# An edge network's segment sum: the row of place numbers written by TensorE into half a bank, and the comparison moved ahead

## The chip, the core and the metric

The kernel runs on one core of one Trainium2 chip. The core has TensorE (PE; its weight loads are shown as PEld), VectorE (DVE), ScalarE (ACT), GpSimd (POOL) and the queues that start transfers, SyncE's (SP) above all. The metric is the device time of one execution in microseconds, the median of several runs. [...]

## The reference

`reference` is one layer of a graph network over 12500 nodes and 212500 edges. Cut to what matters:

```python
h = jnp.maximum(_layernorm(x, axis=-1), 0.0)
edge_in = jnp.concatenate([h[row], h[col], dist], axis=1)
e = jax.nn.silu(edge_in @ eW1 + eb1)
e = jax.nn.silu(e @ eW2 + eb2)
agg = jax.ops.segment_sum(e, row, num_segments=h.shape[0])
node_in = jnp.concatenate([h, agg], axis=1)
out = x + jax.nn.silu(node_in @ nW1 + nb1) @ nW2 + nb2
```

In the call `row` is `src`, in random order of nodes, and `col` is `dst`, by which the edges are sorted.

## The kernel before, in words

**Two halves that overlap.** The first half takes the edges in their order, 208 blocks of 1024. For each block it forms the part of the first product that belongs to `dst` (matmul `qp`, line 459), copies it on ACT into `qs` together with a number (line 477), and POOL sends each 128 rows to a place in a DRAM table `q` that is ordered by the bucket of `src` (line 484). There are 100 buckets of 125 nodes; the places are counted on DVE and PE (`count`, lines 376 to 441: `oh`, `each`, `mine`, `rank`, `to` on DVE, `counts` on PE). A row of `q` has 144 columns: 128 of data and, in column 128, the edge's place: the number of its `src` node within the bucket, 1 to 125, or 0 for an empty row.

The second half reads `q` in steps. A step is four tiles of 128 edges, one of each of four neighbouring buckets; there are 18 levels of 25 steps, 450 in all. The tile `qt` of a step is loaded by SP in `fetch` (line 535), from a pool `ld2` of four buffers. A step's work, by function:

- `s_lr` (567): PE takes the place column of each of the four tiles, spread over 125 columns as the stationary operand, against the identity `identb`. The result, `lr`, has the edges' places along its columns, the same on all 125 partitions: four float32 pieces of 128 columns that fill one bank.
- `s_one_t` (576): DVE compares `lr` with the partition's number, giving `oneT` (node by edge).
- `s_pt` (581): PE transposes `qt` into `pt` and adds the rows `a` of the first product that belong to `src`, picked by `oneT`; ACT applies the first silu (`e1`).
- `s_bias`, `s_p2` (616, 622): ACT puts the second bias in PSUM, PE adds the second product, ACT applies silu (`e2`).
- `s_one` (600): DVE compares the node numbers `nodes1` (in SBUF) with the place column of `qt`, giving `one` (edge by node). At its end it calls `fetch` for four steps later.
- `s_seg` (632): PE sums `e2` over the edges of each node, with `one`, into the only bank `seg`; `s_add` (641) adds it on DVE to `aggT`.

**The order is written by hand.** PE, DVE, ACT and SP run exactly in the order of the program. The list `turn` (line 657) gives it: in turn k the functions are called one after another for steps k plus the number beside them. `None` is a hook, where pieces of the first half (three a block), the node products and the last nodes' work are woven in.

```python
turn = [
    (s_pt, 1), (s_add, -2), (s_one_t, 2), None, (s_bias, 1), (s_p2, 0), (s_one, 0), None, (s_seg, -1), None, (s_lr, 3), None,
]
```

So `lr` of a step comes three turns ahead of its number, `oneT` two, `pt` one, and `one` in its own turn, followed by `seg` a turn later. `lr`, `pt`, `qp` and other short-lived results share the pool `mm` of four banks, in the order in which they are asked for. A tile's buffer goes to its next user when its last reader is done; SP's load of `qt` waits in SP's order for that.

**Kept rows.** The rows `a` are held in SBUF for as many groups of four buckets as fit: `FIRST_KEPT` names those that are kept from their making on, and groups up to `LAST_KEPT` are loaded once and kept. The others are loaded anew at each level (`a`, line 557).

Of the kernel before, what the change touches and what calls it, by code (L numbers as in the profile page):

```python
# [28 lines left out]
F32 = mybir.dt.float32  # L29
F16 = mybir.dt.float16  # L30
BF16 = mybir.dt.bfloat16
# [7 lines left out]
P = 128  # L39
L = 125  # L40
# [11 lines left out]
G = 4  # L52
W = 144
# [6 lines left out]
ROWS = ENDS[-1]  # L60
CAP = ROWS // P
FIRST = 4
FIRST_KEPT, LAST_KEPT = (0, 2, 5, 7, 10, 12, 15, 17, 20, 22), 24
ZP, ZB = 96, 5
FILL0, FILL_EACH, FILL_LATE = 18, 2, 8
AFTER = mybir.DependencyInfo(mybir.DependencyClass.Sync, mybir.DependencyReason.DATA)
# [8 lines left out]
def tile_gnn(ctx: ExitStack, tc: tile.TileContext, x, src, dst, ew, eW1, eb1, eW2, eb2, nW1, nb1, nW2, nb2, out):  # L75
    nc = tc.nc
    N, D = x.shape
    H = eW2.shape[0]
# [9 lines left out]
    const = ctx.enter_context(tc.tile_pool(name="const", bufs=1))  # L88
# [40 lines left out]
    identb = const.tile([P, P], BF16, name="identb")  # L129
# [7 lines left out]
    nodes_i = const.tile([P, L], I32, name="nodes_i")  # L137
# [5 lines left out]
    nodes1 = const.tile([P, L], F32, name="nodes1")  # L143
# [34 lines left out]
    nc.vector.scalar_tensor_tensor(same, plus, -1e6, same, op0=OP.mult, op1=OP.add)  # L178
    ones = const.tile([1, P], F32, name="ones")
    nc.vector.memset(ones, 1.0)  # L180
    before = const.tile([P, P], BF16, name="before")
    nc.vector.tensor_scalar(before, ahead_i, 0.0, float(G), op0=OP.is_gt, op1=OP.mult)
    rest = const.tile([P, P], BF16, name="rest")
# [113 lines left out]
    wk = ctx.enter_context(tc.tile_pool(name="wk", bufs=2))  # L297
# [3 lines left out]
    with ExitStack() as work:  # L301
        mm = work.enter_context(tc.tile_pool(name="mm", bufs=4, space=PSUM))
# [202 lines left out]
        def send_all(s0, s1):  # L505

            for s in range(s0, s1):
                load(s + 2)
                i, rest = divmod(s - FILL0, FILL_EACH)
                if rest == 0 and 0 <= i < len(fills):  # L510
                    fill(*fills[i])

                for j, _ in enumerate(itertools.zip_longest(send(s), count(s + 1))):
                    pending[needed[s]] -= j == PIECES - 1
                    yield
# [3 lines left out]
        steps = [(w, B, n, g) for w, B, n in batches for g in range(n)]  # L519
        PIECES = 1 + TB // G  # L520
        pending = [needed.count(w) for w in range(len(LEVELS))]
        batch, st = {}, {}
# [3 lines left out]
        def fetch(i):  # L526
            if i >= len(batches):
                return
            c, B, n = batches[i]
            assert not any(pending[: c + 1])  # L530
            while B not in done_a:
                next(feed)
            at = B * G * ROWS + G * (ENDS[c] - n * P)
            qt = ld2.tile([P, G * most, W], F32, name="qt")
            ins = nc.sync.dma_start(
                qt[:, : G * n, :].rearrange("p j w -> p (j w)"),
                q[at : at + G * n * P, :].rearrange("(p j) w -> p (j w)", p=P),
            ).ins
            for later in range(c + 1, len(LEVELS)):
                tc.declare_no_dep(ins, group=f"rows{later}", reason="these ranks were full before")  # L540
            tc.add_manual_dep(ins, last_rows[LEVELS[c][1] - 1].name, AFTER)
            tc.add_to_no_dep_group("loads", ins)
            if c == len(LEVELS) - 1 and not ndp:
                kept.clear()
                keeping.close()
                holding.close()
                for name, bufs in (("nd_in", NQ + 5), ("nd", 2), ("al", NQ)):
                    ndp.append(work.enter_context(tc.tile_pool(name=name, bufs=bufs, side="right")))
            a = kept.get(B)
            if a is None:  # L550
                if lap and not ndp and B <= LAST_KEPT:
                    a = kept[B] = lap[0].tile([P, G, H], F32, name=f"al{B}")
                elif ndp:
                    a = ndp[2].tile([P, G, H], F32, name="a_last")
                else:
                    a = ld2.tile([P, G, H], F32, name="a", bufs=NQ - 1)
                nc.sync.dma_start(a, ta_buckets[:, B * G : B * G + G])
            batch[c, B] = [qt, a, None]
            if c == len(LEVELS) - 1:
                node_in[B] = nodes_in(B, ndp[0])  # L560

        def of(k):

            c, B, n, g = steps[k]
            return batch[c, B], [((g * G + t) % n * G + (g * G + t) // n, (g * G + t) // n) for t in range(G)]

        def s_lr(k):
            (qt, _, _), tiles = of(k)
            loc = qt.rearrange("p j w -> p (j w)").bitcast(BF16)
            lr = mm.tile([P, G, P], F32, name="lr", tag="mm")  # L570
            for t, (j, _) in enumerate(tiles):
                at = 2 * (j * W + H) + 1
                nc.tensor.matmul(lr[:L, t, :], loc[:, at : at + 1].to_broadcast([P, L]), identb, start=True, stop=True)  # L573
            st[k] = {"lr": lr}

        def s_one_t(k):
            oneT = wk.tile([L, G, P], F32, name="oneT")
            nc.vector.tensor_scalar(oneT, st[k].pop("lr")[:L], part1[:L, :], None, op0=OP.is_equal)  # L578
            st[k]["oneT"] = oneT

        def s_pt(k):

            (qt, a, _), tiles = of(k)
            oneT = st[k].pop("oneT")
            pt = mm.tile([P, G, P], F32, name="pt", tag="mm")
            for t, (j, _) in enumerate(tiles):
                nc.tensor.matmul(  # L587
                    pt[:, t, :], qt[:, j, :H], ident, is_transpose=True, start=t == 0, stop=False, skip_group_check=True
                )
            for b, same in itertools.groupby(range(G), lambda t: tiles[t][1]):  # L590
                same = list(same)
                cols = slice(same[0], same[-1] + 1)
                nc.tensor.matmul(  # L593
                    pt[:, cols, :], a[:L, b, :], oneT[:, cols, :], start=False, stop=True, skip_group_check=True
                )
            e1 = wk.tile([P, G, P], F32, name="e1")
            nc.scalar.activation(e1, pt, AF.Silu)  # L597
            st[k]["e1"] = e1

        def s_one(k):  # L600
            (qt, _, _), tiles = of(k)
            c, B, n, g = steps[k]
            wide = [P, G // n, n, L]
            loc = qt[:, : G * n, H : H + 1].rearrange("p (j b) w -> p b j w", b=G)
            one = wk.tile([P, G, L], F32, name="one")
            nc.vector.tensor_tensor(  # L606
                one.rearrange("p (b j) l -> p b j l", j=n),
                nodes1[:, None, None, :].to_broadcast(wide),
                loc[:, tiles[0][1] : tiles[0][1] + G // n].to_broadcast(wide),
                op=OP.is_equal,  # L610
            )
            st[k]["one"] = one
            if g == n - 1:
                fetch(c * (NB // G) + B + NQ)

# [25 lines left out]
        def s_add(k):  # L641
# [13 lines left out]


        turn = [
            (s_pt, 1), (s_add, -2), (s_one_t, 2), None, (s_bias, 1), (s_p2, 0), (s_one, 0), None, (s_seg, -1), None, (s_lr, 3), None,
        ]
        hooks = sum(1 for s in turn if s is None)  # L660
        def norm(xs, n, early=False):
# [279 lines left out]
        for _ in range(2):  # L941
            p2 = p2p.tile([P, G, H], F32, name="p2")
            nc.tensor.matmul(p2, ones, b2r, start=True, stop=True)
            nc.scalar.copy(b2f, p2)
        ld2 = work.enter_context(tc.tile_pool(name="ld2", bufs=NQ))
        ndp, lap = [], []
        pieces = send_all(2 * FIRST, nblocks)
        LEAD = 3 * PIECES
# [12 lines left out]
        for w in range(1, len(LEVELS)):  # L961
            start = w * (NB // G) - NQ
# [3 lines left out]
        at = 0  # L966
        for k in range(first, len(steps) + 2):
            for s in turn:
                if s is None:
# [13 lines left out]
                    if tails:  # L983
                        both = tails[at % 2 :: 2][:1] if len(tails) > 1 else tails[:1] * (at % 2)
# [153 lines left out]
```

## Time and profile before

| | |
|---|---|
| median of 3 runs | 3019.96 us (3005.09 to 3024.86) |
| the profiled execution: its own time | 3021.01 us |
| the profiled execution: its span | 3019.2 us |
| mean granted TensorE clock in it | 0.857 |
| PE's share of the chain that ended last | 47% |
| steps; PE matmul instructions | 450; 17391 |

The profile is of one execution. In a row of a group stand the line, the engine, the operation, what it writes and reads, its shape and count; then the busy time of all of them together in us and the mean of one in ns; then the engine's idle time just before them and what ended most of it. Matmuls overlap, so busy time over count is less than the mean. A float32 matmul has two records. The chain of waits is followed back from the last instruction: each piece is what the next one waited for, so a group's share of it is what would be felt if the group took longer. "issue" in it is time in which nothing that the profile shows was waited for. A row of the list of waits reads: engine, line, what ended the wait, then us in total, how often, and the longest; SPq is SP's transfer queue. A row of the timeline or of the chain by time begins with its start and its duration in us.

### The profile page before, as it was taken

Reading aid. Unit: us, or ns where it says so; the run is one execution under the profiler, and the core shown is the slowest. Engines: PE = TensorE matmul, PEld = TensorE weight load, DVE = VectorE, ACT = ScalarE, POOL = GpSimd, SP = SyncE. Lnnn points to the kernel's source line nnn. Section 1 sums busy time; section 2 is a strip of 40 time slices with the busy share of each in tenths; the row PEclk is TensorE's granted clock in tenths of the full one; section 3 lists DMA queues with packets and bytes.
Section 4 is the critical chain, followed back from the end, with each engine's and each line's share of the span. In section 5 each row is a group of like instructions: output and inputs, shape, how many; then the busy total and the mean of one; then the engine's idle time right before and its main releaser. Section 6 shows DMA issues by size and latency. Waiting matters only on the chain.

```text
span 3019.2 us, 48740 instructions
## 1 busy us (share of the span) xinstructions
PE 2356.1 (78%) x17391; PEld 2089.8 (69%) x17391; DVE 1876.5 (62%) x3250; ACT 1096.6 (36%) x2428; POOL 1702.2 (56%) x1712
## 2 busy tenths in 40 slices
PE   2754777778788788888877877887878887878998
PEld 1543566667777777677776767777767776768898
DVE  7653555666667666666665666666666666666555
ACT  2432333333334343333333333333333333434443
POOL 5666556656555555556565665665655556655310
PEclk8555778889989898988898989898888899989999
DMA  4545555444444344444444434444443333333374
GB/s 104 179 156 166 165 177 158 140 133 139 121 125 135 122 139 136 130 127 133 128 142 122 137 120 132 138 136 128 141 131 118 99 110 104 110 99 108 94 226 128
DMA packets 244985, 402.85 MB, mean 133 GB/s; under 512 B 49516, under 2 KB 143647, under 8 KB 244529
## 3 DMA queue, kind: packets, MB, share of 16 engines
q1 hardware_dynamic: 151717, 217.57, 24.5%
q0 software_dynamic: 53536, 123.03, 11.9%
q10 hardware_dynamic: 39482, 59.04, 6.7%
q8 instruction: 140, 2.29, 0.3%
q14 instruction: 110, 0.90, 0.1%
HBM read 192.46 MB, written 207.01 MB: 132 GB/s over the span
## 4 chain that ended last, share of the span: by engine, by line
PE 47%; issue 9%; another core or an unknown queue 8%; DVE 8%; POOL 4%; ACT 2%; DMA 1%; DVEq 0%; POOLq 0%; ACTq 0%; SPq 0%
PE seg L639 10%; PE pt L593 10%; PE p L625 10%; PE pt L587 5%; PE qp L459 5%; POOL q L484 4%; PE lr L573 3%; DVE aggT L650 2%; DVE oneT L578 1%; DVE one L606 1%; DVE mine L434 1%; ACT e L597 1%; DMA qt<-q 1%; PE z L279 1%
## 5 line engine op out<-in xcount | busy, mean ns | idle before, releaser
L484 POOL DMA_INDIRECT q<-qs,to x1661 | 1671.4, 1006 | 1171.5 <-ACT qs L477 655.7
L597 ACT ACTIVATE e<-pt 128x512 f32<-128x512 f32 x450 | 269.4, 599 | 1210.9 <-remote 424.9
L650 DVE TENSOR_TENSOR aggT<-aggT,seg 128x500 f32<-128x500 f32 x425 | 285.7, 672 | 616.7 <-remote 266.3
L639 PE MATMUL seg<-one,e 128*128 128x125 f32 x3600 | 545.9, 297 | 118.5 <-DVE aggT L650 49.5
L625 PE MATMUL p<-w,e 128*128 128x128 f32 x3600 | 564.6, 300 | 62.9 <-issue 53.5
L639 PEld LDWEIGHTS seg<-one,e 128*128 128x128 f32 x3600 | 493.2, 211 | 169.9 <-issue 133.5
L625 PEld LDWEIGHTS p<-w,e 128*128 128x128 f32 x3600 | 508.8, 214 | 100.6 <-issue 83.7
L578 DVE TENSOR_SCALAR oneT<-lr,part 125x512 f32<-125x512 f32 x450 | 335.8, 746 | 114.8 <-remote 29.6
L459 PE MATMUL qp<-win,pick 64*128 64x256 f32 x1662 | 326.3, 461 | 95.2 <-issue 53.4
L629 ACT ACTIVATE e<-p 128x512 f32<-128x512 f32 x450 | 269.8, 599 | 289.2 <-remote 115.0
L587 PE MATMUL pt<-ident,qt 128*128 128x128 f32 x1800 | 311.3, 297 | 35.1 <-issue 23.4
L593 PE MATMUL pt<-oneT,al 125*128 125x128 f32 x1944 | 303.7, 300 | 34.2 <-issue 33.4
L473 ACT COPY qs<-qp 128x512 f32<-128x512 f32 x416 | 243.5, 585 | 216.8 <-PE qp L459 73.0
L459 PEld LDWEIGHTS qp<-win,pick 64*128 64x128 f32 x1662 | 189.4, 214 | 168.8 <-issue 111.7
L593 PEld LDWEIGHTS pt<-oneT,al 125*128 125x128 f32 x1944 | 276.5, 216 | 42.0 <-issue 41.9
L606 DVE TENSOR_TENSOR one<-nodes,qt 128x500 f32<-128x500 f32 x450 | 303.6, 675 | 0.0
L434 DVE TENSOR_TENSOR mine<-oh,counts 128x800 f32<-128x800 bf16 x208 | 204.2, 982 | 159.8 <-remote 90.9
L619 ACT COPY p<-b2f 128x512 f32<-128x512 f32 x450 | 268.4, 596 | 0.0
L587 PEld LDWEIGHTS pt<-ident,qt 128*128 128x128 f32 x1800 | 214.2, 154 | 57.7 <-issue 41.9
L593 PE MATMUL pt<-oneT,ae 125*128 125x128 f32 x1360 | 212.2, 294 | 43.1 <-issue 41.9
L573 PEld LDWEIGHTS <-qt 128*125 128x125 bf16 x1800 | 176.8, 150 | 85.7 <-issue 72.7
L573 PE MATMUL lr<-identb,qt 128*125 128x128 bf16 x1800 | 196.0, 234 | 45.7 <-issue 21.8
(156 smaller groups left out, 1826.7 us busy)
## 6 DMA issues: line engine op xcount, KB each, us to landing
qt<-q SPq DMA_DIRECT2D x450, 288.0 KB
q<-zeros ACTq DMA_DIRECT2D x70, 720.0 KB
q<-qs,to POOLq DMA_INDIRECT x1661
bc<-dests SPq DMA_DIRECT2D x103, 128.0 KB
win<-tb SPq DMA_DIRECT2D x416, 30.0 KB
tb<-got SPq DMA_DIRECT2D x25, 256.0 KB
a_last<-ta SPq DMA_DIRECT2D x25, 256.0 KB
zd<-zn SPq DMA_DIRECT2D x25, 250.0 KB
```

What stands on the lines that cost most here:

```text
L459: nc.tensor.matmul(qps[i][:, t, : n_of[t]], pick[at, t * P : (t + 1) * P], win[at, : n_of[t]], start=True, stop=True)
L484: ins = nc.gpsimd.indirect_dma_start(out=q[:], out_offset=bass.IndirectOffsetOnAxis(ap=to[:k, j : j + 1], axis=0), in_=qs[:k, t, a, :], in ...
L573: nc.tensor.matmul(lr[:L, t, :], loc[:, at : at + 1].to_broadcast([P, L]), identb, start=True, stop=True)
L578: nc.vector.tensor_scalar(oneT, st[k].pop("lr")[:L], part1[:L, :], None, op0=OP.is_equal)
L587: nc.tensor.matmul(pt[:, t, :], qt[:, j, :H], ident, is_transpose=True, start=t == 0, stop=False, skip_group_check=True)
L593: nc.tensor.matmul(pt[:, cols, :], a[:L, b, :], oneT[:, cols, :], start=False, stop=True, skip_group_check=True)
L597: nc.scalar.activation(e1, pt, AF.Silu)
L606: nc.vector.tensor_tensor(one.rearrange("p (b j) l -> p b j l", j=n), nodes1[:, None, None, :].to_broadcast(wide), loc[:, tiles[0][1] : ti ...
L625: nc.tensor.matmul(p2[:, t, :], e1[:, t, :], w2, start=False, stop=t == G - 1, skip_group_check=True)
L629: nc.scalar.activation(e2, p2, AF.Silu)
L639: nc.tensor.matmul(item[2][:, b, :], e2[:, t, :], one[:, t, :], start=j < G, stop=j >= G * (n - 1))
L650: nc.vector.tensor_tensor(v, v, seg, op=OP.add)
```

## The change

Three things are done. In `s_lr` the four matmuls become transposes whose output is bfloat16, so that `lr` takes half of its bank, and a fifth matmul, of one row of ones against one row with the numbers 1 to 125 (`onesb`, `rowb`), writes the node numbers into the other half, as float32, the same on all partitions: `row`. `s_one` is called from `s_one_t`, right after `oneT`, so two steps earlier than before; it reads `row` in place of `nodes1` and has a pool of four buffers, `onep`, in place of two. The call of `fetch` stays where it was, in a function of its own, `s_fetch`. To make room, group 22 is no longer kept from its making on, and group 24 is no longer kept at all.

```diff
-FIRST_KEPT, LAST_KEPT = (0, 2, 5, 7, 10, 12, 15, 17, 20, 22), 24
+FIRST_KEPT, LAST_KEPT = (0, 2, 5, 7, 10, 12, 15, 17, 20), 23
...
+    onesb = const.tile([1, P], BF16, name="onesb")
+    nc.vector.memset(onesb, 1.0)
+    rowb = const.tile([1, L], BF16, name="rowb")
+    nc.vector.tensor_copy(rowb, nodes_i[:1, :])
...
         def s_lr(k):
             (qt, _, _), tiles = of(k)
-            loc = qt.rearrange("p j w -> p (j w)").bitcast(BF16)
-            lr = mm.tile([P, G, P], F32, name="lr", tag="mm")
+            both = mm.tile([P, G * P], F32, name="lr", tag="mm")
+            lr, row = both[:, : 2 * P].bitcast(BF16).rearrange("p (t e) -> p t e", t=G), both[:, 2 * P : 2 * P + L]
             for t, (j, _) in enumerate(tiles):
-                at = 2 * (j * W + H) + 1
-                nc.tensor.matmul(lr[:L, t, :], loc[:, at : at + 1].to_broadcast([P, L]), identb, start=True, stop=True)
-            st[k] = {"lr": lr}
+                loc = qt[:, j, H : H + 1].bitcast(BF16)[:, 1:2]
+                nc.tensor.transpose(lr[:L, t, :], loc.to_broadcast([P, L]), identb)
+            nc.tensor.matmul(row, onesb, rowb, start=True, stop=True)
+            st[k] = {"lr": lr, "row": row}
 
         def s_one_t(k):
             oneT = wk.tile([L, G, P], F32, name="oneT")
             nc.vector.tensor_scalar(oneT, st[k].pop("lr")[:L], part1[:L, :], None, op0=OP.is_equal)
             st[k]["oneT"] = oneT
+            s_one(k)
...
-            one = wk.tile([P, G, L], F32, name="one")
+            one = onep.tile([P, G, L], F32, name="one")
             nc.vector.tensor_tensor(
                 one.rearrange("p (b j) l -> p b j l", j=n),
-                nodes1[:, None, None, :].to_broadcast(wide),
+                st[k].pop("row")[:, None, None, :].to_broadcast(wide),
                 loc[:, tiles[0][1] : tiles[0][1] + G // n].to_broadcast(wide),
                 op=OP.is_equal,
             )
             st[k]["one"] = one
+
+        def s_fetch(k):
+            c, B, n, g = steps[k]
             if g == n - 1:
                 fetch(c * (NB // G) + B + NQ)
...
-            (s_pt, 1), (s_add, -2), (s_one_t, 2), None, (s_bias, 1), (s_p2, 0), (s_one, 0), None, (s_seg, -1), None, (s_lr, 3), None,
+            (s_pt, 1), (s_add, -2), (s_one_t, 2), None, (s_bias, 1), (s_p2, 0), (s_fetch, 0), None, (s_seg, -1), None, (s_lr, 3), None,
...
+        onep = work.enter_context(tc.tile_pool(name="one", bufs=4))
```

## The prediction

> **What bounds the kernel now.** I read the head of the page first, then the chain of waits by line.
>
> ```profile
> span 3019.2 us, 48740 instructions
> PE 2356.1 (78%) x17391; PEld 2089.8 (69%) x17391; DVE 1876.5 (62%) x3250; ACT 1096.6 (36%) x2428; POOL 1702.2 (56%) x1712
> PEclk8555778889989898988898989898888899989999
> PE 47%; issue 9%; another core or an unknown queue 8%; DVE 8%; POOL 4%; ACT 2%; DMA 1%; DVEq 0%; POOLq 0%; ACTq 0%; SPq 0%
> ```
>
> ```profile
> by line: PE seg L639 10.5%; PE pt L593 10.3%; PE p L625 10.2%; issue 9.4%; another core or an unknown queue 8.2%; PE pt L587 5.2%; PE qp L459 5.2%; POOL q L484 4.5%; PE lr L573 2.8%; DVE aggT L650 1.6%; DVE oneT L578 1.3%; DVE one L606 1.0%
> ```
>
> PE makes 47% of the chain and no other engine more than 8%. DVE is busy 62% of the span, but `oneT` and `one` together are 2.3% of the chain. So what PE is given or spared counts nearly in full, and what DVE is given counts little. The second reading is the granted clock: its row moves between 5 and 9 tenths, so PE is often slow after it has stood still, and a stall costs more than its own length. The groups of the touched lines:
>
> ```profile
> L573 PE MATMUL lr<-identb,qt 128*125 128x128 bf16 x1800 | 196.0, 234 | 45.7 <-issue 21.8 <-ACT e L597 11.2 <-DMA qt<-q 9.1
> L587 PE MATMUL pt<-ident,qt 128*128 128x128 f32 x1800 | 311.3, 297 | 35.1 <-issue 23.4 <-ACT e L597 8.8 <-ACT qs L473 1.7
> L625 PE MATMUL p<-w,e 128*128 128x128 f32 x3600 | 564.6, 300 | 62.9 <-issue 53.5 <-ACT p L619 5.1 <-DVE aggT L650 2.2
> L578 DVE TENSOR_SCALAR oneT<-lr,part 125x512 f32<-125x512 f32 x450 | 335.8, 746 | 114.8 <-remote 29.6 <-PE p L625 24.5 <-PE lr L573 16.1
> L606 DVE TENSOR_TENSOR one<-nodes,qt 128x500 f32<-128x500 f32 x450 | 303.6, 675 | 0.0
> L650 DVE TENSOR_TENSOR aggT<-aggT,seg 128x500 f32<-128x500 f32 x425 | 285.7, 672 | 616.7 <-remote 266.3 <-PE seg L639 76.6 <-PE pt L593 64.0
> L396 DVE TENSOR_SCALAR pick<-bc,same,plus 128x512 f32<-128x512 bf16 x102 | 55.3, 542 | 0.0
> L484 POOL DMA_INDIRECT q<-qs,to x1661 | 1671.4, 1006 | 1171.5 <-ACT qs L477 655.7 <-issue 435.1 <-DVE oneT L578 26.2
> ```
>
> DVE is idle 616.7 us ahead of `aggT` alone. That idle time is the cover for everything on DVE below.
>
> **1. The added matmul (`row`).** There are 450 steps, so 450 more weight loads and 450 more bf16 matmuls, of one row of the array. The nearest row is `lr`: 2.8% of the chain is 84.5 us for 1800 of them, 47 ns each on the path. So 450 x 47 = +21 us, which I take, as the two are alike in columns (125 against 128) and type. Ends: 0, where PE is waiting for others anyway, and 450 x 2 x 57 = +51 us, each on the path and at half the clock (57 ns is a fourth of the 0.23 us that four `lr` take in the chain below). Behind it in PE's queue stand hook work and the next step's `pt`; `oneT` waits for the transposes ahead of it, and `aggT` runs on DVE in that time.
>
> ```profile
> 1503.59 0.23 PE lr L573 x4
> 1503.82 0.44 PE pt L587 x4
> ```
>
> **2. Matmuls become transposes.** 1800 for 1800, same operands, output halved. The trace has only float32 transposes, 0.44 us for four, 110 ns each, one record where a float32 matmul of the same size has two (x1800 against x3600). Ends: the present 57 ns, so 0, and 110 ns, so 1800 x 53 = +95 us warm. I take 0: a bfloat16 pass is already one record, and the mode spares float32 its second.
>
> **3. More instructions for PE to fetch.** 17391 matmuls become 17841 (2.6%). The chain's share without any wait that the profile shows, "issue", is 9.4%, 284 us. If it grows with the instructions, 2.6% of it is +7 us, an estimate. Ends: 0 and 15, twice that.
>
> **4. `oneT` from bfloat16.** 512 elements from PSUM cost 746 ns; the nearest bfloat16 source, `pick`, reads 512 from SBUF in 542 ns. Ends: 746, and 542, which is 450 x 204 = 92 us less DVE work. On the path `oneT` is 1.3%, 39 us, so the most to be had is 39 x 204 / 746 = -11 us. I take 0: the output stays float32 and the source stays PSUM, as in the row of `oneT`. [...]
>
> **5. `one` with one operand in PSUM, two steps earlier.** `aggT` has just these operands (one PSUM, one SBUF, 500 elements): 672 ns against 675, so 0 for itself. It moves from behind the first hook to ahead of it. Hook work on DVE in that hook (the counting `oh`, `each`, `mine`, `rank`, `to`, `u`) runs 0.6 us later, and with it PE's `counts` and POOL's sends. Work in the other three hooks does not move. Where DVE stood waiting in the first hook, `one` now fills that wait. I take 0; without the cover it would be all of `one` on the path, 1.0%, 30 us, in either direction. `one` has four buffers and is read three turns later, by `seg`; the buffer it overwrites was read by a `seg` that `aggT`, just ahead of it, has waited for already. No new wait.
>
> **6. POOL is disturbed less.** While `one` reads two SBUF operands a send can stretch:
>
> ```profile
> 1501.53 0.67 DVE L606 TENSOR_TENSOR one<-nodes,qt 128x500 f32<-128x500 f32 x1
> 1501.56 1.48 POOL L484 DMA_INDIRECT q<-qs,to  x1 [0.30 <-issue]
> 1503.34 0.96 POOL L484 DMA_INDIRECT q<-qs,to  x1 [0.30 <-issue]
> ```
>
> A send's mean is 1006 ns against 960 for the undisturbed one here, so all disturbances together are 1661 x 46 = 76 us of POOL. POOL's `q` is 4.5% of the chain, 136 us of 1671 busy, one twelfth. So at most -6 us, and 0 if the two do not touch; I take -3, since `oh` reads two SBUF operands too.
>
> **7. The bank is held longer.** `row` shares the bank of `lr`, so the bank goes back after `one` and not after `oneT`, about 0.67 us later. Four banks go round among `lr`, `pt`, `qp` and others. In a turn with two `qp` the next `lr` gets this one's bank:
>
> ```profile
> 1503.42 0.39 PE L573 MATMUL lr<-identb,qt 128*125 128x128 bf16 x4
> 1505.08 1.14 PE L459 MATMUL qp<-win,pick 64*128 64x256 f32 x8
> 1508.02 0.75 DVE L578 TENSOR_SCALAR oneT<-lr,part 125x512 f32<-125x512 f32 x1 [0.74 <-remote]
> 1509.19 0.39 PE L573 MATMUL lr<-identb,qt 128*125 128x128 bf16 x4
> ```
>
> `one` would end at 1508.02 + 0.66 + 0.67 = 1509.35, so the `lr` of 1509.19 is 0.16 us late. This is one of 21 such cases that I count in the start times of the 450 steps; PE is delayed 8.5 us in all if nothing else moves. I take +5, between 0 and +9.
>
> **8. The edge blocks are loaded earlier.** This is the gain. `one` is today the last reader of the buffer `qt`, and SP's next load of `qt` stands behind it:
>
> ```profile
> SPq L535 <- DVE one L606: 1287.6, 295, 16.1
> SPq L535 <- DVE oneT L578: 173.8, 45, 9.8
> PE lr L573 <- DMA qt<-q: 9.1, 6, 4.1
> PEld L573 <- DMA qt<-q: 11.6, 7, 4.3
> ```
>
> ```profile
> 1590.64 0.17 DVE to L438
> 1590.82 0.60 DVE one L606
> 1591.42 0.02 SPq L535
> 1591.44 0.03 issue
> 1591.47 6.38 DMA qt<-q
> 1597.85 0.04 issue
> 1597.90 0.44 PE lr L573 x4
> ```
>
> Here a late `one` made a late load, and `lr` waited for it. After the change `one` runs two turns sooner and the last reader is `pt`, on PE, a turn earlier; the load's place in SP's order stays, so SP waits for `pt`, or for the transfers ahead of it (`pick` waits for DVE in its own turn, and `win` is issued there too), and the loads behind it on SP go earlier as well. Few of the 450 loads were late, though: the waits on PE sum to 9 to 12 us, and all transfers in the chain are 1%, 30 us. Ends -9 and -30; I take -15, nearer the measured waits. What is late next is `ACT e`, which `lr` waits for at a like rate (11.2 us).
>
> **9. Kept rows.** Bucket group 22 is no longer kept from the start, and 24 is loaded in each of 17 levels: 17 more loads of 256 KB on SP.
>
> ```profile
> L593 PE MATMUL pt<-oneT,a 125*128 125x128 f32 x96 | 17.0, 335 | 0.0
> ...
> DMA packets 244985, 402.85 MB, mean 133 GB/s; under 512 B 49516, under 2 KB 143647, under 8 KB 244529
> ```
>
> At eight records a step, x96 is 12 such loads; they become 29. I take 0: they are needed after `lr`, at the later `pt`, and point 8 moves the loads earlier. Uncovered they cost 17 x 0.26 MB at the mean 133 GB/s, +33 us.
>
> **Sum.** 21 + 0 + 7 + 0 + 0 - 3 + 5 - 15 + 0 = +15 us on the profiled execution's 3021.0 us, 1.1 us above the median of the three runs (3020.0). So 3035 us, a change of 0.5%, below the about 1% that a measurement of this kernel can tell from no change.
>
> **Rivals.**
>
> ```profile
> core 0: 3019.2 us, clock 0.857
> ```
>
> *The loads pay in full, and the clock with them (faster).* All 30 us of point 8 go instead of 15, POOL gives 6, and with fewer stalls the mean granted clock, 0.857, rises to 0.88. PE's 47% of the chain is 1419 us; 0.857 / 0.88 takes 37 us off it. 15 - 15 - 3 - 37 = -40, so 2980. For it: loads gated by `one` 295 times. Against: the waits on PE are few, and most long stalls in the chain are not loads. It decides once loads and clock together give 45 us more than I take.
> [...]
> *A bfloat16 transpose takes as long as a float32 one (slower).* 95 us warm, of which `lr`'s path share, 84.5 of 1800 x 57 = 103 us, is on the path: +78, so 3113. Against it: point 2.
> *The change does nothing on DVE but `oneT` is faster.* -11 us: 3024.
>
> **How the numbers follow.** My forecast, with the faster `oneT` in it, 0.55, and its own range is 3005 to 3065; loads and clock 0.2; clock falls 0.18; slow transposes 0.07. Below 2990 (1% faster) I put 0.15 of the second case and 0.03 of the first, together 0.18; above 3050 (1% slower) 0.15 of the third, all of the fourth and 0.04 of the first, 0.26; between, 0.56. The range takes in the second case's own time and all of the third's, and leaves out what lies past them: half of the second and the fourth, some 0.18. So 2980 to 3090.
>
> **What would show it.** Right: a new PE group of 450 bf16 matmuls and `lr` still at about 0.23 us for four; `oneT` near 746 and `one` near 672 ns; SP's load of `qt` no longer waiting for `one`, and `lr` no longer for `DMA qt<-q`; sends shorter than 1006 ns in the mean. Wrong: a mean granted clock off 0.857 by more than 0.01, four transposes over 0.3 us, new waits of `lr` or `qp` on `one`, or an `aggT` that PE waits for longer.

## The result and the profile after

The changed kernel takes 3099.89 us, the median of four runs (3087.17 to 3102.69), against 3012.53 us for the kernel before (four runs, 2998.74 to 3024.86): ratio 1.0283 [1.0224, 1.0342], so 2.8% slower, above the forecast of 3035 and above the range of 2980 to 3090. Ratios, here and below, leave out executions in a slower state, so they can differ a little from the quotient of two medians; the brackets hold the 95% interval. The profiled execution took 3099.34 us. Head of its page and its chain:

```profile
span 3097.6 us, 49809 instructions
...
PE 2481.1 (80%) x17841; PEld 2153.1 (70%) x17841; DVE 1881.8 (61%) x3252; ACT 1098.2 (35%) x2428; POOL 1658.9 (54%) x1712
...
PEclk9665878879888888889888888888898998889999
...
PE 64%; another core or an unknown queue 12%; issue 10%; DVE 8%; ACT 4%; DMA 1%; POOL 1%; SPq 0%; ACTq 0%; DVEq 0%; POOLq 0%
```

PE was 47% of the chain and is 64%, and POOL has gone from 4% to 1%. The mean granted clock, 0.865, has not fallen (0.857 before). The groups that the change touches, each shape by itself:

```profile
L488 POOL DMA_INDIRECT q<-qs,to x1661 | 1629.7, 981 | 1291.6 <-ACT qs L481 808.0 <-issue 430.7 <-ACT hr L701 10.1
...
L634 PE MATMUL p<-w,e 128*128 128x128 f32 x3600 | 553.5, 299 | 42.1 <-issue 35.8 <-ACT p L628 2.8 <-ACT e L603 1.5
...
L583 DVE TENSOR_SCALAR oneT<-lr,part 125x512 f32<-125x512 bf16 x450 | 336.1, 747 | 168.8 <-PE seg L648 38.4 <-PE p L634 32.5 <-PE lr L578 26.4
...
L593 PE MATMUL pt<-ident,qt 128*128 128x128 f32 x1800 | 334.4, 310 | 32.4 <-issue 24.9 <-ACT qs L477 6.6 <-PE lr L578 0.3
...
L612 DVE TENSOR_TENSOR one<-lr,qt 128x500 f32<-128x500 f32 x450 | 300.9, 669 | 0.0
...
L577 PE MATMUL lr<-identb,qt 128*125 128x128 bf16 x1800 | 193.7, 232 | 33.7 <-ACT e L603 15.4 <-issue 13.7 <-DMA qt<-q 2.7
...
L578 PE MATMUL lr<-rowb,onesb 1*128 1x125 bf16 x450 | 103.8, 231 | 2.0 <-issue 2.0
```

`oneT` (747 ns), `one` (669), `lr` (193.7 us busy against 196.0) and the sends (981 against 1006) are as the prediction had them. The new row, L578 (the views call its output `lr`, whose bank it shares), looks harmless by its busy time: 231 ns, like one `lr`. What it costs is only seen in the starts on PE's timeline:

```profile
1510.04 0.39 PE L577 MATMUL lr<-identb,qt 128*125 128x128 bf16 x4
1510.36 0.22 PE L578 MATMUL lr<-rowb,onesb 1*128 1x125 bf16 x1
1510.52 0.66 PE L593 MATMUL pt<-ident,qt 128*128 128x128 f32 x4
```

From the first `lr` to `pt` it is 0.48 us, where the prediction's chain had 0.23. Over all such places the median from start to start is 57 ns between two `lr`, 153 ns from the last `lr` to the row, and 155 ns from the row to `pt`; before, `lr` to `pt` was 58 ns. So a step of PE is longer by 153 + 155 - 58 = 250 ns, 112 us in 450 steps, where the forecast took 47 ns each. The waits of SP's queue, then some of PE's:

```profile
SPq L539 <- PE pt L593: 435.0, 147, 7.6
...
SPq L539 <- DVE one L612: 80.7, 91, 2.2
```

```profile
PEld qp L463 <- ACT e L603: 28.5, 19, 4.3
...
PE qp L463 <- ACT e L603: 23.5, 12, 3.9
...
PE qp L463 <- DVE one L612: 6.5, 1, 6.5
...
PE lr L577 <- DMA qt<-q: 2.7, 2, 2.0
```

The loads of `qt` have moved from `one` to PE, and `lr` waits 2.7 us for them instead of 9.1. A wait of PE for `one`, which keeps the bank, is seen once, 6.5 us. What is late next is `e` on ACT, as the prediction said: PE waits 23.5 us for it ahead of `qp` and 15.4 us ahead of `lr`.

### The profile page after: what moved, and what is told of

Same layout as the page of the kernel before. It is cut to its first block, busy times and chain, and to the rows that moved or that the text cites. A ratio compares the mean times of both kernels' runs of the same rounds, so it can differ in the third digit from the quotient of the medians.

```text
span 3097.6 us, 49809 instructions
## 1 busy us (share of the span) xinstructions
PE 2481.1 (80%) x17841; PEld 2153.1 (70%) x17841; DVE 1881.8 (61%) x3252; ACT 1098.2 (35%) x2428; POOL 1658.9 (54%) x1712
## 4 chain that ended last, share of the span: by engine, by line
PE 64%; another core or an unknown queue 12%; issue 10%; DVE 8%; ACT 4%; DMA 1%; POOL 1%; SPq 0%; ACTq 0%; DVEq 0%; POOLq 0%
PE pt L599 13%; PE p L634 13%; PE seg L648 12%; PE qp L463 8%; PE pt L593 8%; PE lr L577 3%; PE lr L578 2%; ACT e L603 1%; DVE aggT L659 1%; DVE oneT L583 1%; PE ab L210 1%; PE counts L405 1%; DVE one L612 1%; ACT qs L477 1%
## 5 line engine op out<-in xcount | busy, mean ns | idle before, releaser
L488 POOL DMA_INDIRECT q<-qs,to x1661 | 1629.7, 981 | 1291.6 <-ACT qs L481 808.0
L648 PE MATMUL seg<-one,e 128*128 128x125 f32 x3600 | 532.1, 293 | 82.5 <-DVE aggT L659 41.8
L634 PE MATMUL p<-w,e 128*128 128x128 f32 x3600 | 553.5, 299 | 42.1 <-issue 35.8
L648 PEld LDWEIGHTS seg<-one,e 128*128 128x128 f32 x3600 | 485.1, 208 | 120.4 <-issue 93.2
L463 PE MATMUL qp<-win,pick 64*128 64x256 f32 x1662 | 355.2, 483 | 125.1 <-issue 57.6
L583 DVE TENSOR_SCALAR oneT<-lr,part 125x512 f32<-125x512 bf16 x450 | 336.1, 747 | 168.8 <-PE seg L648 38.4
L593 PE MATMUL pt<-ident,qt 128*128 128x128 f32 x1800 | 334.4, 310 | 32.4 <-issue 24.9
L463 PEld LDWEIGHTS qp<-win,pick 64*128 64x128 f32 x1662 | 201.7, 223 | 209.5 <-issue 143.2
L612 DVE TENSOR_TENSOR one<-lr,qt 128x500 f32<-128x500 f32 x450 | 300.9, 669 | 0.0
L599 PE MATMUL pt<-oneT,ae 125*128 125x128 f32 x1224 | 198.1, 305 | 35.0 <-issue 29.5
L577 PE MATMUL lr<-identb,qt 128*125 128x128 bf16 x1800 | 193.7, 232 | 33.7 <-ACT e L603 15.4
```

The costliest lines, as they stand in the source:

```text
L463: nc.tensor.matmul(qps[i][:, t, : n_of[t]], pick[at, t * P : (t + 1) * P], win[at, : n_of[t]], start=True, stop=True)
L488: ins = nc.gpsimd.indirect_dma_start(out=q[:], out_offset=bass.IndirectOffsetOnAxis(ap=to[:k, j : j + 1], axis=0), in_=qs[:k, t, a, :], in ...
L577: nc.tensor.transpose(lr[:L, t, :], loc.to_broadcast([P, L]), identb)
L593: nc.tensor.matmul(pt[:, t, :], qt[:, j, :H], ident, is_transpose=True, start=t == 0, stop=False, skip_group_check=True)
L599: nc.tensor.matmul(pt[:, cols, :], a[:L, b, :], oneT[:, cols, :], start=False, stop=True, skip_group_check=True)
L612: nc.vector.tensor_tensor(one.rearrange("p (b j) l -> p b j l", j=n), st[k].pop("row")[:, None, None, :].to_broadcast(wide), loc[:, tiles[ ...
```

## The experiments

A group is what ran together on one chip; ratios are to the kernel before in the same group, and the groups fell on five chips. On three (the first, second and fifth group) the kernel before took 3014 to 3090 us, as in the first measurement; on two (third and fourth) 2400 to 2403. They are called the 3050 us and the 2400 us chips here; only ratios of one group are compared closely. Expectations in us were written against the first measurement (3012.53 us before), so on another chip they are to be read as ratios.

**First group** (before 3089.96 us). Theory A: the loss is PE's passage between a matmul of 128 array rows and one of a single row. Theory B: it is the order, the bank or the transposes.

*The row over 128 array rows.* The same product, with zeros below the first row:

```diff
-    onesb = const.tile([1, P], BF16, name="onesb")
-    nc.vector.memset(onesb, 1.0)
-    rowb = const.tile([1, L], BF16, name="rowb")
-    nc.vector.tensor_copy(rowb, nodes_i[:1, :])
+    onesb = const.tile([P, P], BF16, name="onesb")
+    nc.vector.memset(onesb, 0.0)
+    nc.vector.memset(onesb[:1, :], 1.0)
+    rowb = const.tile([P, L], BF16, name="rowb")
+    nc.vector.tensor_copy(rowb, nodes_i)
```

> The changed kernel, with one edit: the stationary operand of the row matmul has 128 rows, the first of ones and the others of zeros, and its moving operand 128 rows of the numbers, so that the result is the same and the matmul fills all rows of the array. Theory A (the passage between a matmul of 128 rows and one of 1 row costs PE about 0.1 us each way, 0.25 us a step with the matmul itself): from the first transpose of lr to the first of pt it takes 0.29 us and not 0.48; 450 x 0.19 = 87 us of PE, of which some 70% on the path, so about 3035 us, between 3015 and 3050. Theory B (the loss is in the held bank, the order or the transposes, and a fifth matmul costs what one of lr costs): no change, 3085 to 3105.

Measured: 3163.51 us, 1.0216 [1.0192, 1.0241]. Its timeline:

```profile
1507.51 0.39 PE L578 MATMUL lr<-identb,qt 128*125 128x128 bf16 x4
1507.74 0.22 PE L579 MATMUL lr<-rowb,onesb 128*128 128x125 bf16 x1
1507.79 0.61 PE L594 MATMUL pt<-ident,qt 128*128 128x128 f32 x4
```

The passage is gone (medians 58 and 55 ns), as A said, and the loss is not: A's 3015 to 3050 us are ratios of 1.001 to 1.012, B's 3085 to 3105 are 1.024 to 1.031, and the measured 1.0216 is nearer to B. A accounts for PE's time, but not for the kernel's.

*No row.* `one` reads `nodes1` in SBUF again, the row's matmul is left out; order, transposes and kept rows stay.

```diff
-            nc.tensor.matmul(row, onesb, rowb, start=True, stop=True)
...
-                st[k].pop("row")[:, None, None, :].to_broadcast(wide),
+                nodes1[:, None, None, :].to_broadcast(wide),
```

> The changed kernel without the row matmul: one is compared with nodes1 in SBUF as before, still right after oneT and two steps earlier, and lr is still made of bfloat16 transposes. Theory A: the whole of the row goes, 450 x 0.25 = 112 us of PE, some 80 us on the path: about 3015, 3000 to 3035; POOL's mean send goes back to about 1006 ns. Theory B: the order and the bank stay, so 3070 or more.

Measured: 3072.58 us, 0.9933 [0.9892, 0.9974]. Order, loads, transposes and kept rows together gain 0.7%, 21 us. The 3072.58 us only look like B's 3070: that figure is a ratio of 1.019, and A's 3000 to 3035 are 0.996 to 1.007. B falls, but for the bank, which goes back early here.

*The row added to the kernel before*, written into `lr`'s bank ahead of `lr`, which overwrites it; then the same over 128 array rows.

```diff
+            nc.tensor.matmul(lr[:, 0, :L], onesb, rowb, start=True, stop=True)
```

> The kernel before, with the row matmul of one row added ahead of lr, into the first piece of lr's bank, where lr overwrites it: the output is the same and nothing reads the row. Theory A: 450 x 0.25 us on PE, some 70 to 90 us on the path: 3080 to 3105. Theory B: a fifth matmul of 57 ns: 3025 to 3040.

> As the kernel before with the added row matmul that lr overwrites, but with 128 rows, as in the first of these kernels. Theory A: 57 ns a step, 26 us of PE: 3025 to 3040. Theory B: the same as with one row.

Measured: 3119.53 us, 1.0116 [1.0083, 1.0150], and 3124.33 us, 1.0119 [1.0086, 1.0151]. The first one's timeline:

```profile
1507.79 0.22 PE L575 MATMUL lr<-rowb,onesb 1*128 1x125 bf16 x1
1507.94 0.44 PE L578 MATMUL lr<-identb,qt 128*125 128x128 bf16 x4
```

One needs about 250 ns of PE a step, the other 55, and both cost 1.2%, 36 us. A expected 1.022 to 1.031 for the first and 1.004 to 1.009 for the second, B 1.004 to 1.009 for both; only B's "the same" came true. On this chip PE's time and the kernel's time do not follow one another. Within this group, the row over 128 array rows costs 1.2% where nothing reads it, and the kernel that also reads it is 2.8% above the one without a row; if the two add up, reading is worth some 1.6%.

**Second group** (before 3089.79 us). Theory C: time saved on PE comes back as standing still and half clock. Theory D: the bank that is held until `one` costs the rest.

> The changed kernel again, on the same chip as the three that follow, since runs on different chips differ by 2 to 3%. Both theories: its ratio to the kernel before is 1.02 to 1.03; it is the yardstick of this group.

> The changed kernel, but one reads nodes1 in SBUF; the row matmul is still issued in its place, and nothing reads its result. So lr's bank is free after oneT, and POOL is disturbed as before. If the cost is PE's own (theory A): as the changed kernel, within 15 us. If it is the bank that one holds longer, and one's wait for the row (theory D): nearer the variant without the row, 40 us or more below the changed kernel.

> The changed kernel without the row matmul, one reading nodes1, and one issued ahead of oneT in place of behind it: lr's bank is freed about 0.65 us later, as in the changed kernel, with no work added on PE. The variant without the row had a ratio of 0.993 to the kernel before. Theory D: 1.010 or more. Theory A: 0.990 to 1.002.

> The changed kernel with the row matmul on 128 rows of the array in place of 1, for the second time. Theory A (the passages between 128 rows and 1 are on the path): 60 to 90 us below the changed kernel on this chip. Theory C (PE's queue is shorter by 86 us, but PE then stands still more and runs longer at half the clock, so the time goes back to waits): within 25 us of the changed kernel, with a mean granted clock lower by 0.01 or more.

The first is the changed kernel and the last the one with 128 array rows. In "row unread" only the operand of `one` is `nodes1` (the second hunk above), so the row is written and not used. "Bank held" is the kernel without a row with the call `s_one(k)` ahead of `oneT`, so that `oneT`, `lr`'s last reader, and the bank come 0.67 us later:

```diff
         def s_one_t(k):
+            s_one(k)
             oneT = wk.tile([L, G, P], F32, name="oneT")
...
-            s_one(k)
```

Measured: changed 3188.13 us, 1.0346 [1.0294, 1.0399]; 128 rows 3176.10, 1.0298 [1.0252, 1.0345]; row unread 3129.70, 1.0146 [1.0104, 1.0189]; bank held 3093.71, 1.0033 [0.9991, 1.0074]. Leaving the row unread gives back 58 us, 2.0%, as D expected (40 us or more). With 128 rows the kernel is 12 us faster than the changed one, where A expected 60 to 90, and the profile's granted clock is 0.845 against 0.851: C's time came true, its fall of the clock by 0.01 only in part. Bank held, at 1.0033, lies between A's 0.990 to 1.002 and D's 1.010 or more, so for chips of this kind D is not settled. Groups and waits of the changed kernel in this group:

```profile
L488 POOL DMA_INDIRECT q<-qs,to x1661 | 1628.7, 981 | 1387.2 <-ACT qs L481 890.7
```

```profile
PE seg L648 <- DVE aggT L659: 72.5, 41, 4.2
...
PE qp L463 <- ACT e L603: 37.5, 14, 6.6
...
PE qp L463 <- DVE one L612: 7.2, 1, 7.2
```

and of the one with the row unread:

```profile
L488 POOL DMA_INDIRECT q<-qs,to x1661 | 1669.6, 1005 | 1256.4 <-ACT qs L481 757.9
```

```profile
PE seg L648 <- DVE aggT L659: 46.8, 33, 3.3
...
PE qp L463 <- ACT e L603: 8.3, 4, 4.1
```

Reading the row makes POOL's sends shorter by 24 ns each, and still the kernel is slower: PE waits 26 us more for `aggT` and 29 us more for `e` ahead of `qp`. The wait for the bank itself is 7.2 us. These say where time is lost, not why.

**Third group** (before 2403.20 us, a 2400 us chip): row or no row, crossed with the order of `one` and `oneT`.

> Two by two in one group, on one chip: the row matmul (issued or not, read by nothing) and lr's bank (freed after oneT, or 0.65 us later because one is issued ahead of oneT); one reads nodes1 in all four. Here: row issued, bank free after oneT. Theory A (the row's time on PE is the cost, the bank is none): this and the next one alike, both about 45 to 65 us above the two without a row. Theory D (the held bank costs about 1% by itself): the held ones 25 to 40 us above their partners.

> Row issued, bank held longer. Theory A: as its partner with the bank free, within 12 us. Theory D: 25 to 60 us above it, up to the whole changed kernel (1.028 to 1.035 of the kernel before).

> No row, bank free after oneT. It was at 0.993 of the kernel before on another occasion. Both theories: 0.985 to 1.000.

> No row, bank held longer. Theory A: as its partner with the bank free, within 12 us. Theory D: 25 to 40 us above it.

| | `oneT` first | `one` first, bank held |
|---|---|---|
| row written, unread | 2410.20, 1.0032 [1.0020, 1.0043] | 2387.31, 0.9934 [0.9922, 0.9946] |
| no row | 2391.67, 0.9952 [0.9939, 0.9965] | 2370.96, 0.9859 [0.9845, 0.9873] |

The row costs 18.5 and 16.4 us here, where A expected 45 to 65, though PE does the same 250 ns a step. `one` first, with the bank held, is no loss but a gain of 0.9%; the sends' mean goes from 1014 to 1003 ns with the row and to 1001 without, and 1661 times 11 or 13 ns is 18 or 22 us of the 23 and 21 gained. D falls on this chip.

**Fourth group** (before 2400.41 us, the other 2400 us chip): does reading cost, by the bank or by the operand, and do the transposes?

> The changed kernel as it is, for the group. Every theory: slower than before by 2.2 to 3.5% if the chip is one on which the kernel before takes about 3050 us; if it is one on which it takes about 2400 us, near 0.3 to 1% slower.

> The changed kernel, with the comparison one reading the kept numbers of SBUF; PE still writes the row, and nothing reads it. This part is left out of the work. Theory E (what is left over beside the row's PE time is the reading of the row out of the bank by one): 1.5 to 2% under the changed kernel of this group, as in the group before. Theory F (the two programs only differ in their luck of layout and power): within 0.7% of the changed kernel.

> As the one with the unread row, but behind each one VectorE copies one column of the row out of the bank into SBUF, so that the bank is let go only behind one, with the wide operand of one still in SBUF. Theory E1 (reading costs because the bank is let go later): as slow as the changed kernel of this group, 1.5 to 2% over the unread row. Theory E2 (reading costs because the wide operand is in PSUM): as the unread row, plus at most 0.3% for 450 small copies on VectorE.

> The kernel before with its four lr matmuls made into bfloat16 transposes into the first half of the same bank, nothing else changed. If the transposes are free, as the prediction had it: within 0.4% of the kernel before, lr at 56 to 57 ns from start to start, and the granted clock the same. If they are dearer in the clock: over 1% slower, with a lower granted clock.

The second new edit lets the bank go only behind `one`, with `one`'s operand still in SBUF; the last is the kernel before with the transposes alone:

```diff
+            seen = onep.tile([P, 1], F32, name="seen")
+            nc.vector.tensor_copy(seen, st[k].pop("row")[:, :1])
```

```diff
-            lr = mm.tile([P, G, P], F32, name="lr", tag="mm")
+            both = mm.tile([P, G * P], F32, name="lr", tag="mm")
+            lr = both[:, : 2 * P].bitcast(BF16).rearrange("p (t e) -> p t e", t=G)
...
-                nc.tensor.matmul(lr[:L, t, :], loc[:, at : at + 1].to_broadcast([P, L]), identb, start=True, stop=True)
+                nc.tensor.transpose(lr[:L, t, :], loc[:, at : at + 1].to_broadcast([P, L]), identb)
```

Measured: changed **2366.49 us, 0.9857 [0.9838, 0.9877]**; row unread 2408.43, 1.0033 [1.0019, 1.0047]; row touched 2409.50, 1.0042 [1.0025, 1.0058]; transposes 2399.77, 1.0001 [0.9990, 1.0013]. On this chip the change is 1.4% faster, which no theory of mine expected, and reading the row, which cost 2.0% on a 3050 us chip, gains 42 us, 1.7%. The page of the changed kernel here:

```profile
span 2365.6 us, 49809 instructions
...
PE 2125.5 (90%) x17841; PEld 1908.2 (81%) x17841; DVE 1853.0 (78%) x3252; ACT 1099.4 (46%) x2428; POOL 1669.6 (71%) x1712
...
PEclk9676789999999999999999999999999999999999
...
PE 61%; DMA 13%; POOL 9%; DVE 8%; issue 5%; ACT 2%; DVEq 0%; SPq 0%; ACTq 0%; POOLq 0%
```

Its sends, and then those of the kernel with the row unread:

```profile
L488 POOL DMA_INDIRECT q<-qs,to x1661 | 1640.5, 988 | 548.0 <-issue 390.3 <-ACT qs L481 51.3 <-DMA q<-qs,to 45.1
```

```profile
L488 POOL DMA_INDIRECT q<-qs,to x1661 | 1681.7, 1012 | 546.7 <-issue 390.2 <-DMA q<-qs,to 48.2 <-ACT qs L481 46.6
```

24 ns less for each of 1661 sends is 40 us, nearly all of the 42. That POOL sets the pace on this chip is read from one stretch of 300 us; the columns are busy us and instructions of PE, PEld, DVE, ACT and POOL, then clock, DMA share and GB/s. On the 2400 us chip the changed kernel and the one with the row unread, and after them the changed kernel of the first measurement:

```profile
1000.00:1300.00 300.00, 285.58 (x2492) 259.92 (x2492) 256.68 (x452) 146.83 (x320) 228.86 (x233) 0.99 0.58 177
```

```profile
1000.00:1300.00 300.00, 278.01 (x2374) 251.78 (x2372) 244.60 (x430) 140.82 (x305) 231.11 (x227) 0.98 0.55 167
```

```profile
1000.00:1300.00 300.00, 255.25 (x1874) 223.21 (x1873) 185.50 (x316) 107.30 (x230) 159.58 (x165) 0.87 0.42 126
```

A send has 0.3 us before it in which POOL waits for nothing that the profile shows. With 233 of them, 228.86 + 70 = 299 of the 300 us are POOL's, and with 227 longer ones 231.11 + 68 = 299: it is full in both. With 165, 159.58 + 50 = 209: it has 30% to spare. The records of all sends bear this out. In all eight profiles of the 2400 us chips no pause before a send is over 0.33 us between 300 and 1900 us; on the 3050 us chips the longest there are 7 to 10 us. And in every profile of this case the kernel ends 150 to 167 us after the last send: here that send ends at 2206 us with the row read and at 2246 unread, 40 of the 42 us. PE is busy for 95% of the stretch too, and has 61% of the chain; but 112 us less work for PE is worth only 16 to 19 us on such a chip, while the time follows the sends. The touched row leaves the sends at 1014 ns and the time at that of the unread row: there it is the operand's place, not the bank, that matters.

The sends go with the operand's place: 1012 ns with `one` on two SBUF operands, 988 with one of them in PSUM. In the first measurement it is seen send by send: in the kernel before, the 306 sends that overlap `one` by over 0.2 us took 1082 ns in the mean and those that don't touch it 987; in the changed kernel it is 966 (291 sends) and 985. Beside `oh`, which still has both operands in SBUF, 167 sends of the changed kernel took 1015 ns in the mean, and those away from it 977. How an operand's place on DVE comes to bear on POOL, no run here shows.

**Fifth group** (before 3013.99 us, a 3050 us chip): the row over 128 array rows again, and the same with `one` first, as the candidate that spares PE and keeps the shorter sends.

> The changed kernel with its row written by a matmul over 128 array rows (a first row of ones over rows of zeros); everything else as it is, the output the same. PE's 112 us a run come back, one still reads the bank, so POOL's sends should take 980 to 990 ns. If the chip takes about 2400 us for the kernel before (POOL's sends and their rows at the end of the chain): 1.5 to 2.5% faster than before. If it takes about 3050 us (half clock and PE's own stops): 1.5 to 3% slower, as in two groups before.

> As the one with the row over 128 array rows, and with one ahead of oneT on VectorE. On a chip of 2400 us: another 0.5 to 1% under the former, as one first gave beside an unread row and without a row. On a chip of 3050 us: within 1% of the former, above it if oneT, which pt waits for, comes 0.67 us later on PE's path, under it if that is hidden.

Measured: 3094.48 us, 1.0245 [1.0191, 1.0299], and 3099.05 us, 1.0286 [1.0243, 1.0329]; no difference that the intervals tell. Neither was tried on a 2400 us chip.

**Where the time stands on the two kinds of chip.** For steps 20 to 440 I took from PE's records the wall time, the gaps (what a time from one matmul's start to the next has beyond 0.25 us, 0.31 behind a `qp`) and the time at half clock. The rest is wall less gaps less half of the half-clock time, an estimate of PE's own work:

| us | wall | gaps | at half clock | rest |
|---|---|---|---|---|
| before, first measurement | 2480 | 517 | 563 | 1682 |
| changed, first measurement | 2555 | 473 | 591 | 1787 |
| no row (first group) | 2512 | 541 | 597 | 1672 |
| 128 array rows (first group) | 2612 | 582 | 700 | 1680 |
| one-row matmul added to the kernel before (first group) | 2554 | 475 | 570 | 1794 |
| the same over 128 array rows (first group) | 2550 | 539 | 628 | 1697 |
| row unread (second group) | 2556 | 486 | 597 | 1771 |
| changed (second group) | 2639 | 541 | 683 | 1757 |
| 128 array rows (second group) | 2628 | 596 | 717 | 1674 |
| row unread (fourth group, a 2400 us chip) | 1955 | 130 | 75 | 1787 |
| changed (fourth group, a 2400 us chip) | 1916 | 104 | 51 | 1787 |
| transposes alone (fourth group, a 2400 us chip) | 1943 | 211 | 96 | 1685 |

The rest hardly depends on the chip: 1672 to 1697 without the one-row matmul and 1757 to 1794 with it, near the 105 us that 420 steps of 250 ns make. The chips differ in gaps and half clock. On the 3050 us chips both rose, within one group, when PE's work was taken away by the 128 array rows (in the changed kernel of the second group gaps 541 to 596 and half clock 683 to 717; in the kernel before with the row added 475 to 539 and 570 to 628) and when the row was read (486 to 541, 597 to 683), and that is where the time went.

## Why the prediction was wrong

The change cost 87 us where the sum had +15. Two steps failed: the price of the added matmul (point 1), and the price of reading its row (points 6 and 7). The signs that the prediction named for being right nearly all came true (`lr`, `oneT`, `one`, the sends, the waits for `qt`, the clock within 0.01), so they could not tell that the time would be missed.

- **Point 1, the added matmul, was mis-sized.** Taken: 47 ns each, because "the two are alike in columns (125 against 128) and type". They differ in array rows, and the passage cost some 97 ns more each way. On PE it is 112 us against +21, past the upper end of +51 too, which was made of the same 57 ns. What the kernel feels is less: 36 us added to the kernel before, 16 to 19 us on a 2400 us chip, and some 2% on the 3050 us chips by a comparison across two groups (1.0146 against 0.9933). This step alone does not make the miss: without the passage the kernel still loses 2.2 to 3.0%.
- **Points 6 and 7, reading the row, are the step that failed most.** I had -3 and +5, together +2. Measured between the row read and unread: +58 us on a 3050 us chip, the kind that the forecast was made for, and -42 us on a 2400 us one. The shorter sends came as forecast, 981 against 1006 ns, and my bound of "at most -6 us" for them came from POOL's 4.5% of the chain, which holds for a chip where POOL has time to spare. Point 7's own mechanism, PE late for the bank, is small: 6.5 and 7.2 us in direct waits. On a 2400 us chip a bank held longer costs nothing (touched row 2409.50 us against 2408.43 with the row unread; `one` first 2387.31 against 2410.20); on a 3050 us chip that is not settled, since bank held came out 1.0% above the kernel without a row of another group.
- **Point 8, earlier loads, fits, but was not tried alone.** Taken: -15. PE's wait of `lr` for the loads fell from 9.1 to 2.7 us as forecast. With the row left out, the new order gains 21 us on a 3050 us chip and 11.5 on a 2400 us one, with points 2 and 9 in it; what share the loads have is not shown.
- **Point 2, the transposes, was right**: 1.0001 by themselves, and `lr`'s 57 ns from start to start did not change. The fall of the clock, to which the forecast gave 0.18, is shown by no run: the mean clock is 0.946 with the transposes alone in a group where the kernel before has 0.942 to 0.958, and 0.865 in the changed kernel against 0.857. Alone the transposes were run on a 2400 us chip only; on a 3050 us chip the kernel without a row, which has them too, had a mean clock of 0.855 against 0.850 before.
- **Points 4 and 5 had the durations right** (747 and 669 ns); that the hook work behind `one` costs nothing was not tried alone. **Point 3** can't be told apart: "issue" in the chain goes from 9.4% to 9.7%, 284 to 300 us, which +7 may be part of, but in the second group it is 8% in the changed kernel and 10% with the row unread. **Point 9** is in the gain of the kernel without a row and was not tried alone.

On the 3050 us chips the parts are: no row -0.7%, row unread about +2.1% (across groups), row read +2.0%; they add up to the second group's 3.5% by construction. Within the first group the row costs +1.2% and reading some +1.6%. On the 2400 us chips: -11.5, +18.5 and -42 us, together -35, against the measured 2366.49 - 2400.41 = -34. The sum on the 2400 us chips closes. On the 3050 us chips the sizes are measured, but not the cause of the third: that reading the row raises gaps and half-clock time is shown in one pair of kernels on one chip (the two of the first group with 128 array rows, read and unread, point the same way, gaps 539 to 582 and half clock 628 to 700, but differ in order too); why it does is open. The touched row, which separates bank and operand, ran on a 2400 us chip only.

## What to carry to other kernels

Price a small matmul by the starts of its neighbours on the timeline, and look at the number of array rows on both sides, not at columns and type alone: here the matmul of one row took some 250 ns a step, the same over 128 array rows 55. Ask of each chip which engine is full: the same shorter sends were worth 42 us where POOL had 299 of 300 us, and bought no time that could be seen where it had 209. When a kernel is near half clock and standing still for part of its time, time saved on one engine need not come out at the end (the 128 array rows took 83 us off the estimate of PE's own work in the second group, and 12 us off the time), and a change of 1 to 3% can have either sign on another chip (1.0283 and 1.0346 on 3050 us chips, 0.9857 on a 2400 us one).

## What the runs showed of the hardware that was not expected

**The same program takes 2400 or 3050 us, by the chip.** On the 3050 us chips PE stands still inside a group of matmuls that waits for nothing that the profile shows. A stretch of the changed kernel's first profile:

```profile
1017.85 1.06 PE L599 MATMUL pt<-oneT,al 125*128 125x128 f32 x8
...
1020.80 0.55 PE L577 MATMUL lr<-identb,qt 128*125 128x128 bf16 x2
1021.85 0.32 PE L577 MATMUL lr<-identb,qt 128*125 128x128 bf16 x2 [0.50 <-issue]
...
1022.25 0.33 PE L593 MATMUL pt<-ident,qt 128*128 128x128 f32 x1
1023.26 0.49 PE L593 MATMUL pt<-ident,qt 128*128 128x128 f32 x3 [0.68 <-issue]
1024.71 2.06 PE L599 MATMUL pt<-oneT,ae 125*128 125x128 f32 x8 [0.96 <-DVE each L394]
```

PE starts again at 1021.85, 1023.26 and 1024.71, 1.41 and 1.45 us apart, and the eight matmuls behind them take 2.06 us where those of 1017.85 took 1.06: the granted clock is 0.5 in the records from 1024.49 to 1027.90 and 1.0 from 1014.25 until then. (The profile puts the third start down to `each` on DVE, which `pt` doesn't read; that it belongs with the two others is read from its distance.) The trace has 382 starts that come 0.5 to 1.6 us after their neighbour within one group in the kernel before and 372 in the changed one, and 20 in each of two profiles of the 2400 us chip. In the changed one, 160 of the 200 that follow another within 3.2 us do so at 0.71 or 1.42 us, to 0.06. In steps 20 to 440, with a pause of over 5 us taken as the end of a spell, they form 125 and 133 spells, half of them 1 to 4 us long, at a median of 15.5 and 14.1 us from one to the next. On the 2400 us chip, in the changed kernel, the group of `p` has no idle time at all:

```profile
L634 PE MATMUL p<-w,e 128*128 128x128 f32 x3600 | 481.0, 276 | 0.0
```

The granted clock is 1.0 or 0.5 in the records of both profiles of the first measurement, never between, and 229 of the 230 pieces before and 261 of the 262 after the change are whole multiples of 3.41 us. Of the 113 falls to 0.5 in steps 20 to 440 of the changed kernel's profile, 76 come within 6 us after the start of such a spell, where only 31% of all moments lie so close; 4 us after a start the clock is at half in 56% of the cases, 1 us before it in 7%. In the kernel before it is 67 of 100 falls, with 30% of all moments so close, and 50% against 6%; so far the prediction's reading of the clock row, that PE is often slow after it has stood still, is borne out. For two thirds of the falls the stops come first and the half clock follows; that the one brings the other is not tested. What sets the spacing of 0.7 and 1.4 us, and why the 2400 us chips have so few of these starts, no run here shows.

**The passage between 128 array rows and one** costs the same on both kinds of chip: 153 to 155 ns from start to start on either side of the row, against 55 to 58 with 128 rows throughout.
